# Layer 1's feed-forward: the last norm scaled with tokens on partitions instead of transposed twice

## The chip, the cores and the metric

The kernel runs on one core of one Trainium2 chip. The metric is the device time of one execution in microseconds (us), of which the profile shows the part that it calls the span. A core has a matrix engine (TensorE, PE in the profile, its weight loads PEld), a vector engine (VectorE, DVE), an activation engine (ScalarE, ACT), a general engine (GpSimd, POOL), and a queue for transfers (SP). They run side by side, each in its own program order, and wait for one another by semaphores.

## The reference

Thirty-two images of 3 x 256 x 256 go through a patch tokenizer (256 tokens of 256 features for each image), layer 0 (attention, then a feed-forward on selected tokens) and layer 1 (attention, then a feed-forward with experts). The change lies in the last: with `h` the tokens of an image, `x` its layer norm, four heads (NH) of 64 features (HD), four experts (NE) in each head:

```python
sx = einsum('bsh,ndh->bnsd', x, hl_w) + hl_b
q = einsum('bnsd,neod->bneso', sx, wq); k = einsum('bnsd,nod->bnso', sx, wk); v = einsum('bnsd,nod->bnso', sx, wv)
att = softmax(einsum('bnesd,bntd->bnest', q, k) * d ** 0.5 + causal)
qkv = einsum('bnest,bntd->bnesd', att, v)
gs = softmax(einsum('bnsf,nef->bnse', out, gate_w) + gate_b)        # out: the experts' qkv side by side
mixed = einsum('bnsed,bnse->bnsd', out, gs)
hn = layernorm(mixed + resid, ln_g, ln_b)                           # over 64 features
hx = relu(fx @ fc1_w.T + fc1_b) @ fc2_w.T + fc2_b                   # fx: hn by head
hx = layernorm(hx + fx, fnorm_g, fnorm_b)                           # the last norm
fg = softmax(fout @ fgate_w.T)                                      # fout: hx, heads side by side
result = h + fout * fg                                              # one factor of fg for each head
```

## The kernel before

All is float32, with tokens or features on the 128 partitions. An image has 256 tokens, so two chunks (NC = 2) of 128. The residual `H[b]`, two chunks by 256 features, stays in SBUF from the tokenizer to the end. The stages before layer 1's feed-forward are not touched, but for lines in `prepare`, which makes small weights in passing.

PSUM is used as eight banks of 128 x 512, handed out in turn by `bank()`: who asks for a bank waits until the reader of eight banks earlier is done.

The feed-forward is cut into 59 pieces (`PIECES`), small functions that each work on one image. `ROUND` is a list of (how many images back, piece), written out in full, and a round goes through it once; so pieces of about eight images are interleaved, and every engine gets its instructions in that order (`manual_schedule`). When the last image's scores are reached, the list `END` takes over. All instructions of one engine are thus in a fixed order, and an instruction that waits holds up all behind it on its engine. The pieces of an image:

- `tokens`: the layer norm of `H[b]` without scale and bias, two DVE instructions of 128x256 in `normed`. `turn`, `turned`: transposed by PE, copied by ACT (`exT`).
- `heads`, `heads_out`: `sx`, features on partitions; a copy `sw` with the halves of the partitions exchanged is made by DMA. `heads_zero` counts zeros in it on DVE, as (post, 16) does later in `fxT`.
- `experts`, `experts_out`: `g`, `sx` times the product of an expert's query matrix and the key matrix.
- `head_values`, `head_values_out`: the values of a head, with a few columns beside them: for each expert, EC = 5 columns, which are four for the gate's logits and one that gives the sum of the exponentials. A row of `ev` holds VC = 84 columns: 5 + 5 + 64 + 5 + 5. DVE adds a row of zeros and ones (`ones_row`) on the way from PSUM to SBUF.
- `scores` 0 to 5, `exponentials` 0 to 5 (ACT, `et`), `later_keys` 0 to 5: POOL zeroes what lies behind the causal mask (L1136).
- `outputs` 0 to 7: exponentials times values, for one head and one chunk. `TAKE` says which columns of `ev` an expert takes: 74 or 69, so that a head's four experts are 286 columns of a bank, which ACT copies to `eo` (L1153). `OWN` and `MIX` say where an expert's logits and values are in it.
- (post, 0), (post, 1): reciprocal of the sums, logits of the gate, its exponential on ACT. (post, 2): rest of the softmax on DVE, then POOL multiplies the experts' values by the gates, two instructions of 128x1024 (L1215). (post, 3): DVE adds the experts (`two`, `er`) and the residual. (post, 15), (post, 4): squares on ACT, their sums on DVE, and POOL's power −1/2 (`head_rstd`, L1167). (post, 5): `er` times that (L1233).
- (post, 6), (post, 60): transposed, scaled (`fxT`). (post, 7), (post, 70): first layer, Relu. (post, 8), (post, 80): second layer, with four more columns for each head that carry the logits of the last gate, to `ey`, tokens on partitions, by DVE. (post, 9), (post, 10): squares, sums, power as above.
- (post, 11): `enorm`, `ey` times the power (L1273); the logits of the gate, and its exponential on ACT (`fgate`).
- (post, 12): four transposes of `enorm`; (post, 120): ACT scales and shifts by feature, `foT` (L1286); (post, 13): four transposes back (L1294).
- (post, 14): rest of the gate's softmax (L1178 to L1180), the transposed norm in PSUM times the gate (L1300), plus `H[b]` (L1304), and the DMA to the output.

So the last norm's scale and bias, which go by feature, are applied where features lie on partitions, between two transposes:

```python
im.fT = p1.tile([P, 2, N], F32, name="foT")
nc.scalar.activation(
    im.fT.rearrange("p k n -> p (k n)"), im.pt, AF.Identity, bias=col("fn_b"), scale=col("fn_g")
)
```

Of the kernel before, what the change touches and what calls it, by code (L numbers as in the profile page):

```python
# [33 lines left out]
F32 = mybir.dt.float32  # L34
AF = mybir.ActivationFunctionType
# [44 lines left out]
def vit_tower(tc, a, out):  # L80
# [468 lines left out]

    EC = NE + 1  # L550
    VC = NE * EC + HD
    TAKE = ((0, 2 * EC + HD), (EC, EC + HD), (2 * EC, EC + HD), (2 * EC, 2 * EC + HD))
    OC = sum(w for _, w in TAKE)

    starts = [sum(w for _, w in TAKE[:e]) for e in range(NE)]
    OWN = [starts[e] + (0, EC, 2 * EC + HD, 3 * EC + HD)[e] - TAKE[e][0] for e in range(NE)]
    MIX = [starts[e] + 2 * EC - TAKE[e][0] for e in range(NE)]

# [63 lines left out]
    def prepare():  # L622
# [13 lines left out]
        for o in (NE, EC + NE, 2 * EC + HD + NE, 3 * EC + HD + NE):  # L636
            nc.gpsimd.memset(ones_row[:, o : o + 1], 1.0)
# [38 lines left out]
        for hp in range(2):  # L676
            for k, o in enumerate((0, 2 * EC + HD)):
                w = WV[:, hp, o : o + 2 * EC].rearrange("p (e x) -> p e x", e=2)
                nc.gpsimd.memset(w[:, :, NE:], 0.0)
                nc.vector.tensor_copy(  # L680
                    w[:, :, 0:NE],
                    pv[:, hp * 16 + k * 8 : hp * 16 + k * 8 + 8].rearrange("p (e x) -> p e x", e=2),
                )
# [27 lines left out]
        for hp in range(2):  # L711
            nc.vector.tensor_copy(WV[:, hp, 2 * EC : 2 * EC + HD], wv_i[:, hp, :])
# [39 lines left out]

    def normed_e(pool, b):
        x = pool.tile([P, NC, D], F32, name="ex")
        normed(x, b, st_e)
        return x

    def features(pool, x):
        xT = pool.tile([P, 2, N], F32, name="exT")
        nc.scalar.copy(xT.rearrange("p k n -> p (k n)"), feature_major(x))  # L760
        return xT
# [250 lines left out]
    with (  # L1012
# [13 lines left out]
        def tokens(b, im):  # L1026
            im.x = normed_e(p1, b)
# [70 lines left out]
        def head_values_out(b, im):  # L1098
            im.v = p2.tile([P, NC, NH, VC], F32, name="ev")
            for h, p in enumerate(im.pv):  # L1100
                nc.vector.tensor_tensor(
                    im.v.rearrange("p c (k h) x -> p (c k) h x", h=2)[:, :, h, :],
                    p[:, 0 : 2 * NC * VC].rearrange("p (g x) -> p g x", x=VC),
                    over(ones_row, [P, 2 * NC, VC], 1), ALU.add,
                )

# [34 lines left out]
        def outputs(b, im, j):  # L1141
            if j == 0:
                im.o = p2.tile([P, NC * NH, 360], F32, name="eo")
            n, c = ((0, 0), (1, 0), (0, 1), (1, 1), (2, 0), (3, 0), (2, 1), (3, 1))[j]
            p, o = bank(), 0
            for e in range(NE):
                x, w = TAKE[e]
                for m in range(c + 1):
                    t = im.t[n, e, True] if m else im.t[n, e, False][:, c * P : (c + 1) * P]
                    for q in (slice(0, HD), slice(HD, P)):  # L1150
                        mm(p[q, o : o + w], t[:, q], im.v[:, m, n, x : x + w], m == 0, m == c)
                o += w
            nc.scalar.copy(im.o[:, c * NH + n, 0:OC], p[:, 0:OC])  # L1153
# [33 lines left out]
        def expert_pair(im, k, at, w):  # L1187

            x, step = at[2 * k], at[2 * k + 1] - at[2 * k]
            return im.o[:, :, x : x + 2 * step].rearrange("p g (e x) -> p g e x", e=2)[:, :, :, 0:w]  # L1190

        def post(b, im, i):
# [78 lines left out]
            if i == 11:  # L1271
                im.r = p1.tile(G8, F32, name="enorm")
                nc.vector.tensor_tensor(im.r, im.y[:, :, 0:HD], over(im.rs, G8, 2), ALU.mult)  # L1273
                lg = spool.tile([P, NC, NH, NH], F32, name="lg2")
                nc.vector.tensor_tensor(
                    lg.rearrange("p c n x -> p (c n) x"), im.y[:, :, HD:], over(im.rs, [P, NC * NH, NH], 2), ALU.mult
                )
                im.gate = spool.tile([P, NC, NH], F32, name="fgate")
                nc.vector.tensor_reduce(im.gate, lg.rearrange("p c n x -> p c x n"), AX.X, ALU.add)
                nc.vector.tensor_tensor(im.gate, im.gate, over(fg_row, [P, NC, NH], 1), ALU.add)  # L1280
                softmax_to_exp(im.gate, NC)
            if i == 12:
                im.pt = feature_major(im.r.rearrange("p (c n) d -> p c (n d)", c=NC))
            if i == 120:
                im.fT = p1.tile([P, 2, N], F32, name="foT")
                nc.scalar.activation(  # L1286
                    im.fT.rearrange("p k n -> p (k n)"), im.pt, AF.Identity, bias=col("fn_b"), scale=col("fn_g")
                )
            if i == 13:
                im.po = bank()  # L1290
                for c in range(NC):
                    for k in range(2):
                        o = c * D + k * P
                        nc.tensor.transpose(im.po[:, o : o + P], im.fT[:, k, c * P : (c + 1) * P], ident)  # L1294
            if i == 14:
                softmax_rest(im.gate, NC)

                y = p1.tile([P, NC, D], F32, name="ex" if b > B - 6 and b % 2 else "fout")
                y8 = y.rearrange("p c (n d) -> p (c n) d", d=HD)
                nc.vector.tensor_tensor(  # L1300
                    y8, im.po.rearrange("p (g d) -> p g d", d=HD),
                    over(im.gate.rearrange("p c n -> p (c n)"), G8, 2), ALU.mult,
                )
                nc.vector.tensor_tensor(y, y, H[b], ALU.add)  # L1304
# [10 lines left out]
            (tokens,), (turn,), (turned,), (heads,), (heads_out,), (experts, 0), (head_values,), (experts_out, 0),  # L1315
            (experts, 1), (experts_out, 1), (head_values_out,), (scores, 0), (scores, 1), (exponentials, 0),
            (exponentials, 1), (heads_zero,), (later_keys, 0), (scores, 2), (scores, 3), (scores, 4), (scores, 5),
            (exponentials, 2), (exponentials, 3), (exponentials, 4), (later_keys, 1), (exponentials, 5),
            (later_keys, 2), (later_keys, 3), (outputs, 0), (outputs, 1), (outputs, 2), (outputs, 3),
            (later_keys, 4), (outputs, 4), (outputs, 5), (later_keys, 5), (outputs, 6), (outputs, 7), (post, 0),  # L1320
            (post, 1), (post, 2), (post, 3), (post, 15), (post, 4), (post, 5), (post, 6), (post, 60), (post, 16),
            (post, 7), (post, 70), (post, 8), (post, 80), (post, 9), (post, 10), (post, 11), (post, 12), (post, 120),
            (post, 13), (post, 14),
        )
        ROUND = (
            (1, 39), (0, 24), (0, 25), (-3, 0), (-1, 13), (4, 54), (3, 48), (4, 55), (0, 26), (0, 27), (3, 49),
            (-1, 14), (2, 44), (2, 45), (5, 57), (1, 40), (5, 58), (-2, 3), (2, 46), (-1, 15), (-3, 1), (4, 56),
            (-2, 4), (0, 28), (0, 29), (-3, 2), (0, 30), (0, 31), (3, 50), (3, 51), (1, 41), (0, 32), (0, 33),
            (0, 34), (0, 35), (3, 52), (0, 36), (3, 53), (0, 37), (-2, 5), (-2, 6), (-1, 16), (-2, 7), (0, 38),
            (-2, 8), (-2, 9), (-1, 17), (-1, 18), (-2, 10), (1, 42), (-1, 19), (-1, 20), (2, 47), (-1, 21), (1, 43),  # L1330
            (-1, 22), (-1, 23), (-2, 11), (-2, 12),
        )
        END = (
            (3, 47), (0, 21), (0, 22), (2, 43), (5, 57), (5, 58), (0, 23), (4, 54), (2, 44), (3, 48), (3, 49),
            (0, 24), (1, 39), (0, 25), (2, 45), (2, 46), (0, 28), (0, 29), (1, 40), (0, 26), (1, 41), (2, 47),
            (0, 30), (0, 27), (0, 32), (0, 31), (0, 33), (0, 34), (1, 42), (0, 35), (0, 36), (3, 50), (1, 43),
            (3, 51), (0, 37), (3, 52), (2, 48), (2, 49), (0, 38), (0, 39), (1, 44), (1, 45), (1, 46), (4, 55),
            (0, 40), (3, 53), (4, 56), (0, 41), (3, 54), (4, 57), (2, 50), (1, 47), (2, 51), (1, 48), (1, 49),
            (0, 42), (0, 43), (4, 58), (0, 44), (3, 55), (2, 52), (2, 53), (0, 45), (3, 56), (3, 57), (3, 58),
            (0, 46), (1, 50), (0, 48), (1, 51), (0, 47), (1, 52), (0, 49), (2, 54), (2, 55), (2, 56), (2, 57),  # L1340
            (1, 53), (0, 50), (1, 54), (2, 58), (0, 51), (0, 52), (1, 55), (0, 53), (1, 56), (1, 57), (1, 58),
            (0, 54), (0, 55), (0, 56), (0, 57), (0, 58),
# [411 lines left out]
```

## Time and profile before

| | |
|---|---|
| median of 3 runs | 1951.76 us (1950.18 to 1952.43) |
| the profiled execution | 1953.11 us, span 1951.4 us, mean clock 0.989 |
| busy in the span: PE, PEld | 1908.1 us (98%), 1370.5 us (70%) |
| DVE, ACT, POOL | 1209.3 us (62%), 821.0 us (42%), 877.5 us (45%) |
| from 1240 us on: layer 1's feed-forward | some 710 us |

The shares are means over stages. In the part that the change touches, the feed-forward from about 1240 us to the end, all engines are busier than over the span. Times of instructions are from the profile: a group's mean is the duration of one instruction, but instructions of one engine overlap at their ends, so that the distance from start to start, read from the timeline, is what one costs its engine.

### The profile page before, as it was taken

To read this page: it belongs to the slowest core of one execution; us is meant where nothing else is said; L and a number is where in the kernel's file an instruction comes from. 1 tells how busy PE (TensorE), PEld (TensorE's weight loads), DVE (VectorE), ACT (ScalarE), POOL (GpSimd) and SP (SyncE) were. 2 spreads that over 40 slices of the span, in tenths; PEclk is the share of its full clock that TensorE was granted. 3 is DMA by queue.
4 is the path that set the end of the run, shared out by engine and by line. 5 is a ranking of instruction groups with operands and counts; after the bars stand their busy time and mean duration, and the time that the engine had idled before them with its cause. 6 is when DMAs were issued, how large, how long until landed. Compare 5 with 4: busy or idle time off the path is not lost.

```text
span 1951.4 us, 37903 instructions
## 1 busy us (share of the span) xinstructions
PE 1908.1 (98%) x15108; PEld 1370.5 (70%) x15108; DVE 1209.3 (62%) x3225; ACT 821.0 (42%) x1549; POOL 877.5 (45%) x1072
## 2 busy tenths in 40 slices
PE   9999999999999999999989999999999999999994
PEld 7887676767676767676545555577888888888873
DVE  2334456565656574434365655545788888888886
ACT  0001222121212122212434444367878787878762
POOL 1224224343424252433443343336767676767672
PEclk9999999999999999999999999999999999999996
DMA  8540000000000042221000000011222222222212
GB/s 289 161 148 15 1 17 30 19 22 11 22 12 22 33 140 57 81 62 52 17 11 1 1 1 1 1 23 29 52 55 56 56 54 58 53 60 51 62 51 61
DMA packets 69671, 95.03 MB, mean 49 GB/s; under 512 B 8561, under 2 KB 51057, under 8 KB 69105
## 3 DMA queue, kind: packets, MB, share of 16 engines
q1 hardware_dynamic: 62768, 74.98, 13.4%
q0 software_dynamic: 6144, 16.79, 2.8%
q8 instruction: 121, 1.98, 0.4%
q10 hardware_dynamic: 576, 0.79, 0.1%
q14 instruction: 62, 0.50, 0.1%
HBM read 46.38 MB, written 20.97 MB: 35 GB/s over the span
## 4 chain that ended last, share of the span: by engine, by line
PE 95%; DVE 2%; POOL 1%; DMA 1%; ACT 0%; issue 0%; SPq 0%; ACTq 0%; DVEq 0%
PE bank L115 90%; PE bank L750 2%; PE bank L188 1%; PE bank L1294 1%; DMA patch<-in_patches_dram 0%; POOL hv L1167 0%; PE bank L229 0%; PE bank L482 0%; POOL et L1136 0%; DVE six L123 0%; DMA both<-hx 0%; POOL eo L1215 0%; DVE enorm L1273 0%; DVE ranges L1228 0%; DVE h L827 0%
## 5 line engine op out<-in xcount | busy, mean ns | idle before, releaser
L1136 POOL TENSOR_SCALAR_AFFINE_SELECT et<-et 128x256 f32<-128x256 f32 (+1 forms) x384 | 200.2, 553 | 19.4 <-ACT et L1126 18.8
L115 PE MATMUL bank<-ev,et 128*64 128x74 f32 (+1 forms) x6144 | 205.7, 227 | 1.9 <-POOL et L1136 1.9
L115 PEld LDWEIGHTS bank<-ev,et 128*64 128x64 f32 x6144 | 197.6, 138 | 8.0 <-issue 5.2
L1126 ACT ACTIVATE et<-bank 128x512 f32<-128x512 f32 x384 | 201.0, 660 | 0.0
L115 PE MATMUL bank<-tokW,patch 128*128 128x256 f32 x768 | 169.1, 383 | 2.7 <-DMA patch<-in_patches_dram 2.7
L115 PE MATMUL bank<-g,sx 64*128 64x512 f32 (+1 forms) x512 | 170.7, 483 | 0.0
L115 PE MATMUL bank<-g,sw 64*128 64x512 f32 (+1 forms) x512 | 170.3, 483 | 0.0
L115 PEld LDWEIGHTS bank<-tokW,patch 128*128 128x128 f32 x768 | 147.7, 193 | 24.4 <-issue 3.5
L1153 ACT COPY eo<-bank 128x286 f32<-128x286 f32 x256 | 101.9, 402 | 91.1 <-PE bank L115 78.7
L115 PE MATMUL bank<-bxT,w_wuv 128*128 128x512 f32 x300 | 131.4, 592 | 0.0
L115 PEld LDWEIGHTS bank<-g,sw 64*128 64x128 f32 x512 | 95.7, 187 | 33.0 <-issue 21.9
L148 POOL TENSOR_SCALAR rs_c<-st_c 128x4 f32<-128x4 f32 x16 | 3.1, 191 | 251.8 <-DVE st_c L124 251.8
L1215 POOL TENSOR_TENSOR eo<-eo,gate 128x1024 f32<-128x1024 f32 x60 | 115.2, 1940 | 1.5 <-DVE gate L1212 1.5
L115 PE MATMUL bank<-wvo,dm 128*128 128x512 f32 x256 | 114.3, 599 | 0.0
L115 PE MATMUL bank<-attn,bv 128*128 128x256 f32 x512 | 113.1, 379 | 0.0
L115 PE MATMUL bank<-w_wo,gT 128*128 128x256 f32 x512 | 113.1, 379 | 0.0
L115 PE MATMUL bank<-w_w,hT 128*128 128x256 f32 x512 | 113.1, 379 | 0.0
L115 PE MATMUL bank<-xsel,w_w 128*128 128x512 f32 x256 | 111.4, 592 | 0.0
L1167 POOL TENSOR_TENSOR hv<-hv,minus_half 128x8 f32<-128x8 f32 x64 | 108.8, 1699 | 5.3
L115 PEld LDWEIGHTS bank<-attn,bv 128*128 128x128 f32 x512 | 97.2, 190 | 19.6 <-issue 6.9
L115 PEld LDWEIGHTS bank<-g,sx 64*128 64x128 f32 x512 | 95.7, 187 | 19.4 <-issue 14.8
L123 DVE BATCH_NORM_STATS2 six<-h 128x6 f32<-128x256 f32 x256 | 105.6, 412 | 4.4
(268 smaller groups left out, 3845.6 us busy)
## 6 DMA issues: line engine op xcount, KB each, us to landing
patch<-in_patches_dram SPq DMA_DIRECT2D x31, 768.0 KB, 4.6
sw<-sx SPq DMA_DIRECT2D x64, 128.0 KB, 2.7
both<-fxT SPq DMA_DIRECT2D x64, 128.0 KB, 3.2
both<-hx SPq DMA_DIRECT2D x64, 128.0 KB, 2.4
out_dram<-fout SPq DMA_DIRECT2D x29, 256.0 KB, 2.1
cs<-ranked SPq DMA_DIRECT2D x32, 128.0 KB, 2.0
results<-cy SPq DMA_DIRECT2D x32, 128.0 KB, 1.7
w_w<-in_w_dram SPq DMA_DIRECT2D x2, 1024.0 KB
```

Source lines behind the costliest of these rows:

```text
L115: nc.tensor.matmul(o, lhsT, rhs, start=first, stop=last)
L123: nc.vector.bn_stats(six, x)
L148: nc.gpsimd.tensor_scalar(o, var, 1.0, 1e-5, ALU.mult, ALU.add)
L188: nc.tensor.transpose(p[:, o : o + P], x[:, c, k * P : (k + 1) * P], ident)
L750: nc.tensor.transpose(p[:, o : o + P], x[:, c, k * P : (k + 1) * P], ident)
L1126: nc.scalar.activation(t, p, AF.Exp)
L1136: nc.gpsimd.affine_select(out=own, in_=own, pattern=[[0, n_e], [1, P]], compare_op=ALU.is_ge, fill=0.0, base=0, channel_multiplier=-1,)
L1153: nc.scalar.copy(im.o[:, c * NH + n, 0:OC], p[:, 0:OC])
L1167: nc.gpsimd.tensor_tensor(v, v, minus_half, ALU.pow)
L1215: (nc.vector if b > B - 3 else nc.gpsimd).tensor_tensor(im.mix[k], im.mix[k], over(im.gate[:, :, 2 * k : 2 * k + 2], [P, NC * NH, 2, HD], ...
L1294: nc.tensor.transpose(im.po[:, o : o + P], im.fT[:, k, c * P : (c + 1) * P], ident)
```

## The change

The last norm stays with tokens on partitions. (post, 12), (post, 120) and (post, 13) are gone, and (post, 11) makes no `enorm`. (post, 14) makes, after the gate's softmax, the product of gate and power (`both_factors`, 128x8); then for each of the eight combinations of chunk and head one DVE instruction of 128x64 that multiplies `ey` by its column of `both_factors` and by the row `fn_g`; eight more that multiply the row `fn_b` by the gate and add `H[b]`; and one addition of 128x512 of the two.

The values have a second copy: a row of `ev` is 148 columns (5 + 64 + 5, twice), so that every expert takes 69 columns (WC) and a head's four are 276. `head_values` and its 84 columns in PSUM are as before; `head_values_out` is now three DVE additions (4x74, 4x5, 4x5) and one ACT copy of 4x64 for each of two banks. `MIX` is such that the values of two experts lie side by side in `eo`.

`tokens` runs on ACT (two instructions of 128x256 with scale and bias by token), after one small DVE instruction for the bias (`e_less`).

`PIECES`, `ROUND` and `END` are new. In `ROUND`, (post, 14) follows closely on (post, 2), (post, 80) comes behind it, and `tokens` between them:

```diff
     EC = NE + 1
+    WC = EC + HD
     VC = NE * EC + HD
-    TAKE = ((0, 2 * EC + HD), (EC, EC + HD), (2 * EC, EC + HD), (2 * EC, 2 * EC + HD))
-    OC = sum(w for _, w in TAKE)
...
+    VU = 2 * (WC + EC)
+    TAKE = (0, EC, WC + EC, WC + 2 * EC)
+    OC = NE * WC
...
         def tokens(b, im):
-            im.x = normed_e(p1, b)
+            im.x = p1.tile([P, NC, D], F32, name="ex")
...
+            nc.vector.scalar_tensor_tensor(less, st[:, i, :, 0], -1.0, rs, ALU.mult, ALU.mult)
+            for c in range(NC):
+                nc.scalar.activation(
+                    im.x[:, c, :], H[b][:, c, :], AF.Identity, bias=less[:, c : c + 1], scale=rs[:, c : c + 1]
+                )
...
         def head_values_out(b, im):
-            im.v = p2.tile([P, NC, NH, VC], F32, name="ev")
+            im.v = p2.tile([P, NC, NH, VU], F32, name="ev")
             for h, p in enumerate(im.pv):
...
+                first = WC + EC
                 nc.vector.tensor_tensor(
...
+                    v[:, :, 0:first], p[:, :, 0:first], over(ones_row[:, 0:first], [P, 2 * NC, first], 1), ALU.add
                 )
+                nc.vector.tensor_tensor(
+                    v[:, :, first : first + EC], p[:, :, first : first + EC],
+                    over(ones_row[:, first : first + EC], [P, 2 * NC, EC], 1), ALU.add,
+                )
+                nc.vector.tensor_tensor(
+                    v[:, :, VU - EC :], p[:, :, first + EC :], over(ones_row[:, first + EC :], [P, 2 * NC, EC], 1), ALU.add
+                )
+                nc.scalar.copy(v[:, :, first + EC : VU - EC], p[:, :, EC:WC])
...
             if i == 11:
-                im.r = p1.tile(G8, F32, name="enorm")
-                nc.vector.tensor_tensor(im.r, im.y[:, :, 0:HD], over(im.rs, G8, 2), ALU.mult)
...
-            if i == 12:
-                im.pt = feature_major(im.r.rearrange("p (c n) d -> p c (n d)", c=NC))
-            if i == 120:
...
-            if i == 13:
...
             if i == 14:
                 softmax_rest(im.gate, NC)
...
+                nc.vector.tensor_tensor(both, gate, im.rs, ALU.mult)
+                z = p1.tile(G8, F32, name="enorm")
...
+                for g in range(NC * NH):
+                    nc.vector.scalar_tensor_tensor(
+                        z[:, g, :], im.y[:, g, 0:HD], both[:, g : g + 1], row_e("fn_g"), ALU.mult, ALU.mult
+                    )
+                for g in range(NC * NH):
+                    c, n = g // NH, g % NH
+                    nc.vector.scalar_tensor_tensor(
+                        y[:, c, n * HD : (n + 1) * HD], row_e("fn_b"), gate[:, g : g + 1],
+                        H[b][:, c, n * HD : (n + 1) * HD], ALU.mult, ALU.add,
+                    )
                 nc.vector.tensor_tensor(
-                    y8, im.po.rearrange("p (g d) -> p g d", d=HD),
-                    over(im.gate.rearrange("p c n -> p (c n)"), G8, 2), ALU.mult,
+                    y, y, z.rearrange("p (c n) d -> p c (n d)", c=NC), ALU.add
                 )
-                nc.vector.tensor_tensor(y, y, H[b], ALU.add)
                 nc.sync.dma_start(out[b].rearrange("(c p) d -> p c d", p=P), y)
```

The new round, as (images back: piece), from the fourth entry before (post, 14) to (post, 3), and its end:

```
1:post2  0:outputs1  -1:exponentials0  4:post14  0:outputs2  0:outputs3  0:outputs4  3:post8  2:post6  2:post60
-3:tokens  -2:heads  -2:heads_out  3:post80  3:post9  2:post16  -1:later_keys0  -1:heads_zero  -1:scores1  1:post3
-1:exponentials1  -1:later_keys1  -1:scores2  0:outputs5  -1:outputs0  -1:exponentials2  0:outputs6  3:post10
...
0:post0  3:post11      then, at the head of the next:  1:post1  -1:head_values_out  0:scores4  2:post5
0:exponentials4  0:scores5  -1:scores0  0:exponentials5  0:later_keys4  0:later_keys5
```

## The prediction

> **What bounds the kernel now.** I read the stretches first, then the groups by line and shape inside the steady part, then who waited for whom, then the timelines of VectorE and GpSimd. Stretches of 100 us (busy us of PE, PEld, DVE, ACT, POOL; granted clock; DMA):
>
> ```profile
> 1400.00:1500.00 100.00, 100.00 (x1592) 81.80 (x1591) 85.68 (x200) 79.37 (x174) 70.49 (x93) 1.00 0.22 55
> 1600.00:1700.00 100.00, 100.00 (x1581) 80.85 (x1578) 86.43 (x205) 80.06 (x177) 71.12 (x94) 1.00 0.22 55
> ```
>
> The reader is to see PE without a gap at full clock, and DVE at 86%. The chain of waits repeats one piece at a fixed distance:
>
> ```profile
> 1469.35 16.09 PE bank L115 x290
> 1488.92 16.09 PE bank L115 x290
> ```
>
> 1488.92 − 1469.35 = **19.57 us: one image, one pass of ROUND**. Such pieces stand from 1352 to 1841 us: 26 full rounds. Each us per round is worth 26 us of the end.
>
> Groups of 1300 to 1800 us (25.5 rounds): line, engine, out<-in, count | busy us, mean ns | idle before.
>
> ```profile
> L115 PE MATMUL bank<-ev,et 128*64 128x74 f32 x2456 | 123.2, 229 | 0.3 <-POOL et L1136 0.3
> L115 PE MATMUL bank<-ev,et 128*64 128x69 f32 x2464 | 109.1, 223 | 1.6 <-POOL et L1136 1.6
> L1215 POOL TENSOR_TENSOR eo<-eo,gate 128x1024 f32<-128x1024 f32 x51 | 97.2, 1925 | 1.5 <-DVE gate L1212 1.5
> L1180 DVE TENSOR_TENSOR fgate<-fgate,sm_m 128x8 f32<-128x8 f32 x22 | 42.7, 1939 | 0.7
> L1304 DVE TENSOR_TENSOR fout<-fout,h 128x512 f32<-128x512 f32 x21 | 33.3, 1584 | 0.7
> L1233 DVE TENSOR_TENSOR er<-er,hv 128x512 f32<-128x512 f32 x25 | 28.3, 1133 | 1.8 <-POOL hv L1167 1.8
> L1273 DVE TENSOR_TENSOR enorm<-ey,hv 128x512 f32<-128x512 f32 x23 | 15.7, 683 | 0.0
> L1173 DVE TENSOR_TENSOR fgate<-fgate,sm_m 128x8 f32<-128x8 f32 x23 | 3.8, 167 | 0.8
> ```
>
> Two products of the same shape, 8 elements wide: 167 ns at L1173, 1939 ns at L1180. Two 512 wide: 683 and 1584. The long ones wait inside their own duration. The two timelines (start us, us) show for what; of DVE:
>
> ```profile
> 1489.43 1.58 DVE L1304 TENSOR_TENSOR fout<-fout,h 128x512 f32<-128x512 f32 x1
> ...
> 1506.25 1.94 DVE L1180 TENSOR_TENSOR fgate<-fgate,sm_m 128x8 f32<-128x8 f32 x1
> ```
>
> and of POOL:
>
> ```profile
> 1506.23 3.81 POOL L1215 TENSOR_TENSOR eo<-eo,gate 128x1024 f32<-128x1024 f32 x2
> ```
>
> L1180 starts 0.02 us after POOL's first product with the gates and ends with it; L1304, a round later, waits for the second. This **hidden stall** is (1.94−0.17) + (1.58−0.68) + (1.13−0.68) + some 0.2 at small products = 3.3 us a round. DVE also idles openly (who waited for whom: us in total, times, longest):
>
> ```profile
> DVE ey L1265 <- PE bank L115: 30.3, 23, 5.2
> DVE ranges L1228 <- ACT esq L1184: 24.3, 25, 1.6
> ```
>
> 30.3/25.5 + 24.3/25.5 = 2.1, with small waits 2.3. So DVE's own work, gaps between dependent instructions included, is 19.57 − 3.3 − 2.3 = 14.0 us.
>
> **What the Trainium skill says.** "SBUF — State Buffer", Who interferes with whom: a VectorE instruction with two SBUF inputs and a GpSimd instruction that reads SBUF exclude one another for the whole instruction. The 1.94 against 0.17 us agrees; L1300, with one input in PSUM, runs beside the same POOL product in 0.69. "VectorE: DVE Perf Modes", Rules for kernel authors: the number of chained VectorE instructions is what to keep small. Here 32 elements take 184 ns and 512 take 683: 1.04 ns an element and 0.15 us fixed. "PSUM — Partial Sum Buffer", Specifications: eight banks; the kernel takes all eight in turn, so a late reader stops PE eight banks on. No stall of this kind is in the steady trace of before.
>
> **Part by part, us per round.**
>
> *PE.* Gone: four transposes of `enorm` and four of `foT`, each four 0.44 from start to start: −0.88. Half of the 192 output matmuls go from 74 to 69 columns: 123.2/2456 against 109.1/2464 is 5.9 ns counted alone, but the two forms overlap; from start to start a pair takes 59 against 56 ns: 48 × 3.2 ns = −0.15. PE's floor becomes 19.57 − 1.03 = **18.54**. If the width is not what sets these matmuls, 18.69.
>
> *ACT.* Gone `foT` (start to start 0.66). Added: two normalisations 128x256 (nearest L1059, 0.61, the second 0.37 after the first: 0.8) and two copies of values 128x256 (nearest the `eo` copies, 0.40: 0.75). 15.7 + 0.9 = 16.6: below PE's floor by sum, so I cost it at nothing; the cover goes if ACT is held up, see the third rival.
>
> *POOL.* The same instructions, 13.8 busy.
>
> *DVE.* Gone: `ex` 2 × 0.33, `enorm` 0.60, the gate product from PSUM 0.73: −2.0. `both_factors` +0.2, `e_less` +0.15. Values: two additions of 296 instead of 336 elements, four of 20 at 0.1 each: +0.3. Sixteen products with a pointer scalar, 64 wide. The nearest row is 256 wide:
>
> ```profile
> 1181.56 1.66 DVE L955 SCALAR_TENSOR_TENSOR h<-bank,d_rs,h 128x256 f32<-128x256 f32 x4 [0.84 <-POOL d_rs L149]
> ```
>
> (1.66 − 0.48)/3 = 0.39 from start to start, less 192 × 1.04 ns is 0.19; sixteen are 3.1. Bounds: 0.14 (the second of two 64-wide products at L1201 starts that much after the first), so 2.3; 0.26 if they do not overlap, so 4.2. The last addition replaces L1304's. Sum +1.75: DVE's own work is **15.7** (14.9 to 16.8).
>
> *Stalls.* The instructions on DVE that read two SBUF operands grow by some twenty, and the order puts (post, 14) right behind DVE's part of (post, 2), whose gate starts POOL's two products of 1.92. Behind that gate DVE has a reduction and a reciprocal, 0.4, then only two-input instructions: `fgate`, `both_factors`, sixteen products, the addition. So most of 3.85 is lost: 3.3. Where DVE and POOL both queue, the traces show them alternating (L1233 goes between two selects), so the two selects of (later_keys, 0) that follow cost the products 2 × 0.36 = 0.7; `er` by `hv` 0.45 as now; small products and `two` against other selects 0.5. Sum 5.0 (3.0 to 6.0). The two open waits on PE and ACT disappear, since DVE is now late for them; the wait of (post, 11) for POOL's power, 1.69 after the reduction with some 1.6 of DVE work between, and the wait for ACT's square come to 0.8.
>
> *The round* is 15.7 + 5.0 + 0.8 = **21.5: DVE sets it, not PE**. PE meets it at bank reuse: the banks of (post, 8) wait for (post, 80), which is behind (post, 14) on DVE, and (outputs, 5) takes them again.
>
> *Queues.* On SP the output's DMA waits for the end of (post, 14), and `sw<-sx` stands behind it; its reader is a round on and it lands in 2.7, so nothing. POOL's order behind the products is selects needed half a round on: nothing. `prepare` makes some more small copies and memsets beside a PE that is busy: nothing.
>
> *Fill and drain.* The first rounds have no late pieces: 0. In the drain DVE is the longest engine already (35.6 of the last 52 us): three images × 1.75 more, less the transposes' chain of the last image (from 1940.6 to 1943.8, some 3): +3.
>
> Sum: 26 × (21.5 − 19.57) + 3 = +53 on the profiled execution's 1953.1, which is 1.3 over the median 1951.8: **2005**.
>
> **Rivals.** (1) *PE stays the bound.* DVE's stalls and waits together stay under 18.54 − 15.7 = 2.8 a round; break-even is 3.9. POOL's products must then fall beside the counts of zeros and the PSUM additions instead of the products. 26 × 1.03 = −27, so 1925. For: both engines' sums are below 18.6. Against: 3.3 is lost now with half as many such instructions. (2) *DVE binds mildly*: products at 0.14, and a run of them keeps POOL out instead of alternating: 14.9 + 3.9 + 0.9 = 19.7; with the drain +6, so 1958. (3) *ACT's order adds a loop*: its normalisation waits for `e_less`, which is behind (post, 14) on DVE. From there to the end of (exponentials, 5) ACT has 13.2 of its own, at the start-to-start times of its timeline (five pairs of exponentials at 1.0, four copies of `g` 2.0, four of `eo` 1.6, two squares 1.1, normalisations, `sx` and values 0.8 each, the rest 1.1); then POOL's select 1.3, its products 3.9, DVE's rest of (post, 14) 4.1: 22.5, +79, so 2031. (4) *Narrower matmuls bring nothing*: 4 us at most, inside the others.
>
> **How the numbers follow.** 0.2% (3.9 us) is about what a measurement of this kernel tells from no change. The forecast (rounds of 20.6 to 22.4) has 0.50, rival 1 0.15, rival 2 0.22 (of it 0.03 faster, 0.05 the same), rival 3 0.13. So faster 0.18, same 0.05, slower 0.77. The slower cases' own range is 1960 to 2035; taking in rival 2's fast side (round 19.4) gives 1948 to 2035, leaving out rival 1 and the worst of rival 3.
>
> **What would show it.** Right: rounds of about 21.5 us, PE with gaps of 2 to 3 us a round ahead of (outputs, 5) released by DVE `ey`; one `fgate`, `both_factors` or `enorm` instruction of 1 to 2 us in each round; DVE near 98%. Wrong: PE at 100% and a round of 18.5, or these products all at their short duration; then the stalls were mispriced. `enorm` rows with a step of 0.14 or 0.26 would show that I mis-sized the product.

## The result, and the profile after

The changed kernel takes **2013.93 us** (median of 4 runs, 2012.07 to 2015.08) against 1950.97 us of the kernel before on the same chip (4 runs, 1949.97 to 1952.43): a ratio of 1.0321, with an interval of 1.0303 to 1.0339. The profiled execution has a span of 2013.3 us, 61.9 more than before, and a mean clock of 0.977.

The stretches of the kernel after (us of PE, PEld, DVE, ACT, POOL; granted clock; DMA share; GB/s), one of the steady part and the last one:

```profile
1500.00:1600.00 100.00, 89.80 (x1383) 70.12 (x1383) 92.80 (x269) 72.95 (x171) 61.92 (x82) 0.98 0.22 55
...
1950.00:2014.00 64.00, 20.70 (x300) 15.47 (x296) 48.37 (x175) 10.65 (x24) 14.36 (x15) 0.61 0.17 47
```

PE now has gaps, 10 us in 100, and does 1383 matmuls in 100 us of the steady part where it did 1592. DVE has gone from 86% to 93%. The page's shares of the chain that ended last say the same for the whole span (PE had 95% and DVE 2% before):

```profile
PE 71%; DVE 22%; ACT 4%; issue 1%; POOL 0%; DMA 0%; SPq 0%; ACTq 0%; DVEq 0%; POOLq 0%
```

In the chain of waits of the kernel after (start us, us, what), the piece that repeats is no longer a run of matmuls but (post, 14) on DVE:

```profile
1430.68 5.98 DVE enorm L1297 x8
...
1444.49 0.59 ACT esq L1191
1445.11 0.69 DVE ranges L1236
...
1452.72 5.26 DVE enorm L1297 x8
...
1474.05 5.26 DVE enorm L1297 x8
...
1481.67 0.36 DVE ey L1273
1482.17 5.79 PE bank L115 x98
...
1495.44 5.07 DVE enorm L1297 x5
```

1495.44 − 1430.68 is 64.76 us for three images, 21.6 for one. The eight products take up to 5.98 us. The two lines after the third of them show how DVE holds PE: the addition (post, 80) at L1273 comes behind (post, 14), and PE's output matmuls come behind that addition. In the two rounds before, the chain comes back to DVE through ACT instead, from the normalisation behind `e_less` to a square and its sum (`esq`, `ranges`). That is the loop of rival 3, which "The loop of `e_less`" below looks into. Groups of the kernel after, 1300 to 1800 us (line, engine, out<-in, count | busy us, mean ns | idle before):

```profile
L1297 DVE SCALAR_TENSOR_TENSOR enorm<-ey,both_factors,rows_e 128x64 f32<-128x64 f32 x161 | 112.2, 764 | 0.7
L1302 DVE SCALAR_TENSOR_TENSOR fout<-rows_e,fgate,h 128x64 f32<-128x64 f32 x160 | 32.9, 273 | 0.0
L1306 DVE TENSOR_TENSOR fout<-fout,enorm 128x512 f32<-128x512 f32 x20 | 13.8, 692 | 0.7
L1187 DVE TENSOR_TENSOR fgate<-fgate,sm_m 128x8 f32<-128x8 f32 x21 | 9.8, 467 | 0.7
```

L1297 and L1302 are the same instruction in shape, and one takes 764 ns, the other 273. `fgate` (1939 ns before) and the last addition (1584 before) are now at 467 and 692: most of the stall has moved from them to the products. Why is in the timelines of one round of the kernel after (start us, us); DVE's:

```profile
1516.92 0.62 DVE L1187 TENSOR_TENSOR fgate<-fgate,sm_m 128x8 f32<-128x8 f32 x1
1517.57 0.55 DVE L1292 TENSOR_TENSOR both_factors<-fgate,hv 128x8 f32<-128x8 f32 x1
1518.16 5.26 DVE L1297 SCALAR_TENSOR_TENSOR enorm<-ey,both_factors,rows_e 128x64 f32<-128x64 f32 x8
1523.35 1.64 DVE L1302 SCALAR_TENSOR_TENSOR fout<-rows_e,fgate,h 128x64 f32<-128x64 f32 x8
```

and POOL's:

```profile
1518.08 3.96 POOL L1223 TENSOR_TENSOR eo<-eo,gate 128x1024 f32<-128x1024 f32 x2
1521.99 0.77 POOL L1142 TENSOR_SCALAR_AFFINE_SELECT et<-et 128x256 f32<-128x256 f32 x2
```

From 1518.08 to 1522.76 POOL has two products and two selects, and DVE's first eight products last for all of it. Taken singly, they go 1909, 272, 1929, 433, 436, 272, 272 and 272 ns, beside POOL's 1913 and 1970 (products) and 406 (selects): DVE waits out one POOL instruction, gets one product in, and waits out the next. Where nothing is in the way, products start 0.196 us apart.

### The profile page after: what moved, and what is told of

It reads as the page before. It is cut to its first block, busy times and chain, and to the rows that moved or that the text cites. A ratio compares the mean times of both kernels' runs of the same rounds, so it can differ in the third digit from the quotient of the medians.

```text
span 2013.3 us, 37927 instructions
## 1 busy us (share of the span) xinstructions
PE 1903.8 (95%) x14852; PEld 1350.2 (67%) x14852; DVE 1351.9 (67%) x3805; ACT 833.3 (41%) x1645; POOL 881.9 (44%) x1076
## 4 chain that ended last, share of the span: by engine, by line
PE 71%; DVE 22%; ACT 4%; issue 1%; POOL 0%; DMA 0%; SPq 0%; ACTq 0%; DVEq 0%; POOLq 0%
PE bank L115 69%; DVE enorm L1297 8%; DVE fout L1302 2%; ACT et L1132 1%; PE bank L188 1%; DVE er L1241 1%; DVE ev L1101 1%; DVE fout L1306 1%; ACT eo L1160 1%; ACT esq L1191 1%; DVE ranges L1236 1%; DVE fgate L1187 1%; DVE both_factors L1292 1%; ACT sx L1056 1%; DVE sm_m L1186 1%
## 5 line engine op out<-in xcount | busy, mean ns | idle before, releaser
L1142 POOL TENSOR_SCALAR_AFFINE_SELECT et<-et 128x256 f32<-128x256 f32 (+1 forms) x384 | 206.3, 563 | 193.9 <-ACT et L1132 191.0
L115 PEld LDWEIGHTS bank<-ev,et 128*64 128x64 f32 x6144 | 208.4, 146 | 91.2 <-issue 75.7
L115 PE MATMUL bank<-ev,et 128*64 128x69 f32 x6144 | 217.2, 234 | 54.8 <-DVE ey L1273 54.8
L1132 ACT ACTIVATE et<-bank 128x512 f32<-128x512 f32 x384 | 210.0, 628 | 2.5 <-PE bank L115 2.5
L115 PE MATMUL bank<-g,sw 64*128 64x512 f32 (+1 forms) x512 | 185.4, 492 | 0.0
L115 PE MATMUL bank<-g,sx 64*128 64x512 f32 (+1 forms) x512 | 185.0, 492 | 0.0
L1297 DVE SCALAR_TENSOR_TENSOR enorm<-ey,both_factors,rows_e 128x64 f32<-128x64 f32 x256 | 156.8, 681 | 1.1
L115 PEld LDWEIGHTS bank<-g,sx 64*128 64x128 f32 x512 | 90.7, 187 | 32.8 <-issue 22.9
L115 PEld LDWEIGHTS bank<-w_w,hT 128*128 128x128 f32 x512 | 96.6, 190 | 15.3 <-issue 2.9
```

The lines of the kernel that those rows point to most:

```text
L115: nc.tensor.matmul(o, lhsT, rhs, start=first, stop=last)
L1132: nc.scalar.activation(t, p, AF.Exp)
L1142: nc.gpsimd.affine_select(out=own, in_=own, pattern=[[0, n_e], [1, P]], compare_op=ALU.is_ge, fill=0.0, base=0, channel_multiplier=-1,)
L1297: nc.vector.scalar_tensor_tensor(z[:, g, :], im.y[:, g, 0:HD], both[:, g : g + 1], row_e("fn_g"), ALU.mult, ALU.mult)
```

## The experiments

"Round" is the distance of two images in the steady part of the trace. The stall is summed over DVE's instructions in it: duration less the shortest one of the same form (same operation, same sizes). All ratios are to the kernel before on the same chip.

| kernel | median us | ratio (interval) | round | stall |
|---|---|---|---|---|
| before | 1951 | | 19.57 | 3.6 |
| after | 2013.93 | 1.0321 (1.0303 to 1.0339) | 21.6 | 5.1 |
| tokens_early | 2015.86 | 1.0327 (1.0310 to 1.0344) | 21.7 | |
| norm_alone | 2010.09 | 1.0301 (1.0283 to 1.0318) | 21.4 | 5.9 |
| norm_by_powers | 2043.01 | 1.0473 (1.0455 to 1.0490) | 22.9 | 2.1 |
| norm_by_powers2 | 2012.71 | 1.0314 (1.0297 to 1.0332) | 21.6 | 3.2 |
| mix_short2 | 1939.16 | 0.9951 (0.9934 to 0.9968) | 19.0 | 1.8 |
| rest_alone | 1962.78 | 1.0059 (1.0042 to 1.0076) | 19.8 | |
| wide_norm | 1992.20 | 1.0219 (1.0202 to 1.0236) | 20.9 | 5.4 |
| values_on_dve | 1948.36 | 0.9980 (0.9969 to 0.9990) | 19.4 | |
| mix_dve | 1976.73 | 1.0127 (1.0112 to 1.0143) | 20.2 | 1.6 |
| wide_mix_dve | 1955.61 | 1.0021 (1.0013 to 1.0029) | 19.55 | 1.6 |
| wide_reordered | 1958.21 | 1.0043 (1.0029 to 1.0057) | 19.7 | 1.7 |

Theory 1 is the prediction's: the round is DVE's, by its own work and by its stalls against POOL. What stands against it in the expectations below is theory 2 (DVE's own work sets the round without the stalls), theory 3 (rival 3: the loop of ACT's normalisation behind `e_less`) and theory 4 (the other parts of the change cost).

### Only the last norm: norm_alone

The kernel before, its order and all else kept, with (post, 12), (post, 120) and (post, 13) gone and the new (post, 14) in its old place (three buffers for `ey`, six for `hv`, since both are held longer):

```diff
-            if i == 12: ...          (and 120, 13)
+            if i == 14:              (the softmax, both_factors, 8 + 8 products, one addition, as after)
```

> The kernel before, with only the last norm changed: no transposes, sixteen products and one addition in (post, 14), three buffers for `ey`; the round, the end, `tokens` on DVE, `ev` and the 74 columns as before. Theory 1: DVE's own work 14.0 - 1.3 + 3.3 = 16.0, stalls 4.9 since (post, 14) stands behind (post, 2) here too, waits 0.5: a round of 21.4, some 2001 us (1985 to 2015). Theory 4 (what costs is the new round, or `tokens` on ACT, or the values' second copy): at most 1955, and 1926 if PE still sets the round at 18.7.

2010.09 us, 21.4 a round: this part alone makes all but 4 us of the loss. A stretch of norm_alone, and groups from 1300 to 1800 us:

```profile
1500.00:1600.00 100.00, 93.63 (x1314) 72.45 (x1311) 97.04 (x257) 70.79 (x156) 61.51 (x85) 0.98 0.21 52
```

```profile
L1289 DVE SCALAR_TENSOR_TENSOR enorm<-ey,both_factors,rows_e 128x64 f32<-128x64 f32 x160 | 87.6, 615 | 0.7
L1284 DVE TENSOR_TENSOR both_factors<-fgate,hv 128x8 f32<-128x8 f32 x20 | 37.5, 1875 | 0.7
```

In the old order the first of POOL's products is waited out in `both_factors` (8 elements, 1875 ns), the second in the products. The sum is not smaller for it, 5.9 against 5.1: the stall belongs to whatever two-input instructions stand behind the gate. The run also speaks against theory 3: it has no `e_less`, and the normalisation is DVE's. DVE is at 97%, and the chain of waits from 1400 to 1500 us is made of DVE's instructions alone.

### The other parts: rest_alone and values_on_dve

rest_alone is the kernel before with all of the change but the last norm: the second copy of the values, 69 columns for every expert, values copied and tokens normalised by ACT, all in the old order of pieces.

```diff
-                im.v = p2.tile([P, NC, NH, VC], F32, name="ev")
+                im.v = p2.tile([P, NC, NH, VU], F32, name="ev")
...
+                nc.scalar.copy(v[:, :, first + EC : VU - EC], p[:, :, EC:WC])
```

> The kernel after's other parts without the last norm: values with a second copy, 69 columns for each expert, `tokens` on ACT; the last norm, the pieces, the round and the end as in the kernel before. Theory 1: PE 0.2 us a round less and still without a gap, DVE 0.2 less, ACT 1.5 more but under PE: 1944 to 1950. Theory 4 (these parts cost): above 1960.

A miss: 1962.78 us, slower than before by 0.6%, 19.84 a round. The output matmuls did get 0.19 us a round shorter (6.11 to 5.92 from start to start), but PE lost more than that elsewhere: 0.2 ahead of `heads`, 0.1 within it and 0.2 among the matmuls of the scores. The stretch of rest_alone has ACT at 84%, where it was 79 to 80% before:

```profile
1500.00:1600.00 100.00, 99.81 (x1596) 81.11 (x1592) 77.15 (x215) 84.00 (x192) 68.63 (x90) 1.00 0.23 55
```

values_on_dve tests that: the same, but with the copy and the normalisation on DVE, which has room in the kernel before.

```diff
-                nc.scalar.copy(v[:, :, first + EC : VU - EC], p[:, :, EC:WC])
+                nc.vector.tensor_copy(v[:, :, first + EC : VU - EC], p[:, :, EC:WC])
```

(and `normed` on DVE for `tokens`, as before)

> The kernel before with the values' second copy and 69 columns for each expert, the copy made by DVE instead of ACT; `tokens`, last norm, pieces, round and end as before. In rest_alone PE's output matmuls took 0.19 us a round less and PE lost 0.3 behind ACT. Theory 1: DVE gets 1.0 us a round more (2 x 0.33 and four narrow additions), of 2.3 that it idles; PE stays without a gap, a round of 19.38: 1944 to 1948. If DVE is not free at the places where these stand: 1952 to 1965.

1948.36 us, 0.2% under before (interval 0.9969 to 0.9990), with rounds of 19.38 (a mean of 19.46, since one in eight is 20.1). So narrower output matmuls, with the copy that they need on DVE, are worth some 3 us, and by the two ratios some 15 us lie between the copy and the normalisation on DVE and the same on ACT. Which of the two pieces costs this on ACT was not separated. Of the versions that compute the whole result it is the one that beats both kernels, by about as much as the measurement can tell.

### Without POOL's products: mix_short2

POOL's products are cut short, so that DVE meets next to nothing of them. The kernel leaves out the gates of 63 of 64 columns, and (post, 3) adds `H[b]` to itself in place of the experts' values, with the same sizes and two operands in SBUF; so its output is not the model's, and only its time is of use. (mix_short, with the first of these two edits alone, has no time: some results of the unweighted values were not finite.) All else is as after.

```diff
-                        im.mix[k], im.mix[k], over(..., [P, NC * NH, 2, HD], 3), ALU.mult
+                        im.mix[k][:, :, :, 0:1], im.mix[k][:, :, :, 0:1], over(..., [P, NC * NH, 2, 1], 3), ALU.mult
-                nc.vector.tensor_tensor(two, im.mix[0], im.mix[1], ALU.add)
+                nc.vector.tensor_tensor(two, h8, h8, ALU.add)        # h8: H[b], in the shape of two
```

> The kernel after, but POOL's product of the experts' values with the gates covers 1 of 64 columns, and (post, 3) adds H to itself in place of the experts' values (same shape, same two SBUF operands), so that all numbers stay small. Theory 1 (POOL's two products of 1.9 us hold off the sixteen small products of (post, 14)): the stall inside `enorm` falls from 3.9 us a round to under 1, the round from 21.6 to 18.5 to 19.2 us, the time to 1925 to 1945. Theory 2 (DVE's longer own work sets the round by itself): the round stays above 20.5, the time above 1985.

1939.16 us, 75 less than after, with DVE's instructions the same in number, shape and order. Stretch, group and two pieces of the chain of waits of mix_short2:

```profile
1500.00:1600.00 100.00, 100.00 (x1588) 78.11 (x1584) 87.67 (x306) 85.22 (x192) 50.72 (x90) 1.00 0.22 58
```

```profile
L1299 DVE SCALAR_TENSOR_TENSOR enorm<-ey,both_factors,rows_e 128x64 f32<-128x64 f32 x184 | 60.0, 393 | 0.8
```

```profile
1452.71 10.24 PE bank L115 x180
...
1471.73 10.24 PE bank L115 x180
```

The products are at 393 instead of 764 ns, and PE is without a gap. The chain of waits of the steady part is PE's throughout, so the round of 19.0 is PE's own. Theory 2 falls with it. Theory 3 does not: POOL's products are a member of rival 3's loop too. They took 0.24 us each here, 3.4 less in all, and 22.5 less 3.4 is 19.1. Against it stands norm_alone, and the next run tests that loop in the new order.

### The loop of `e_less`: tokens_early

```diff
 ROUND, as (images back: piece):
-        1:post2  0:outputs1  -1:exponentials0  4:post14  ...  2:post60  -3:tokens  -2:heads
+        -3:tokens  1:post2  0:outputs1  -1:exponentials0  4:post14  ...  2:post60  -2:heads
```

> The kernel after with one piece moved in the round: `tokens` stands ahead of (post, 2), so that `e_less` is no longer behind (post, 14) on DVE and ACT does not wait for it (4 us a round in the kernel after). Theory 1: ACT's wait is a consequence; the round stays at 21.7 and the time within 6 us of 2014. Theory 3 (the loop through `e_less`, ACT, the exponentials and POOL sets the round): 1 us a round or more is gained, 1990 or less.

2015.86 us, no gain. In the waits of after (engine line waited for: us in total, times, longest) the normalisation stands high; it is a wait of ACT, 1300 to 1850 us:

```profile
ACT ex L1022 <- DVE e_less L1020: 100.1, 23, 5.3
PE bank L115 <- DVE ey L1273: 43.3, 22, 2.9
DVE ranges L1236 <- ACT esq L1191: 20.5, 23, 2.6
```

In tokens_early the first line is gone. ACT now waits for `ey` of (post, 80), which stands behind the same (post, 14) on DVE:

```profile
ACT esq L1191 <- DVE ey L1273: 73.8, 22, 4.2
PE bank L115 <- DVE ey L1273: 44.4, 22, 2.9
```

So ACT is still held by DVE, and this run takes only one entrance of the loop away. How much ACT's lateness can cost is in the third line of after: DVE stands idle for ACT's squares 20.5 us in some 25 rounds, 0.8 us a round, and in the steady part, apart from 0.5 for PE at `ev` and the gaps between dependent instructions, it is never without an instruction. A round longer by 2.1 us than before cannot come from 0.8. ACT's wait was slack behind DVE, not what set the round; PE's wait for `ey` is as long as it was.

### POOL's products on DVE: mix_dve, wide_norm, wide_mix_dve

mix_dve gives the two products with the gates to DVE, which has the most to do already. It is the sharpest test of the stall: DVE's own work rises by more than 2 us a round.

```diff
-                    (nc.vector if b > B - 3 else nc.gpsimd).tensor_tensor(
+                    nc.vector.tensor_tensor(
```

> The kernel after with the two products of values and gates on DVE for every image, nothing else. Theory 1: DVE's own work 16.1 + 2.3 = 18.4, stalls against the selects 1.0 to 1.8, waits 0.5: a round of 19.9 to 20.7, 1962 to 1985, faster than the kernel after although DVE has more to do. Theory 2: 21.6 + 2.3, above 2060.

1976.73 us, 37 less than after, with more work on the engine that bounds. Groups of mix_dve, 1300 to 1800 us:

```profile
L1223 DVE TENSOR_TENSOR eo<-eo,gate 128x1024 f32<-128x1024 f32 x50 | 71.3, 1426 | 1.7
L1297 DVE SCALAR_TENSOR_TENSOR enorm<-ey,both_factors,rows_e 128x64 f32<-128x64 f32 x176 | 38.8, 287 | 0.8
```

The two products cost DVE 2.85 a round, what they wait for included, and the eight products of `enorm` are back at 287 ns. The stall goes from 5.1 to 1.6, and the gaps between DVE's instructions from 1.7 to 1.4; with 1.4 less for the round that leaves 2.4 more of own work.

wide_norm takes the other term, DVE's own work: five 512-wide instructions instead of sixteen products and an addition.

```diff
-                for g in range(NC * NH):
-                    nc.vector.scalar_tensor_tensor(z[:, g, :], im.y[:, g, 0:HD], both[:, g : g + 1], row_e("fn_g"), ALU.mult, ALU.mult)
-                for g ...                                      (fn_b times the gate, plus H[b])
+                nc.vector.tensor_tensor(z, im.y[:, :, 0:HD], over(both, G8, 2), ALU.mult)
+                nc.vector.tensor_tensor(y8, over(row_e("fn_b"), G8, 1), over(gate, G8, 2), ALU.mult)
+                nc.vector.tensor_tensor(z, z, over(row_e("fn_g"), G8, 1), ALU.mult)
+                nc.vector.tensor_tensor(y, y, H[b], ALU.add)
```

> The kernel after with the sixteen products of 64 columns and the addition as five instructions of 512 columns: 0.6 to 0.7 each against 16 x 0.196 + 0.75. Theory 1: DVE's own work 0.7 us a round less, and as DVE sets the round, so is the round, with stalls of 4 to 5 as before: 20.6 to 21.2, 1985 to 2003. If the number of instructions queued against POOL sets the stall (fewer hand-overs): down to 19.8, 1965. Theory 3 (a loop through ACT sets it): 2010 or more.

1992.20 us, 20.86 a round, 0.77 less than after. The stall stays, 5.4; now it sits in the first two of the five:

```profile
L1298 DVE TENSOR_TENSOR fout<-rows_e,fgate 128x512 f32<-128x512 f32 x21 | 49.0, 2335 | 0.0
L1297 DVE TENSOR_TENSOR enorm<-ey,both_factors 128x512 f32<-128x512 f32 x21 | 48.5, 2311 | 0.7
```

So DVE's own work taken away comes off the round, and fewer instructions do not make the stall smaller: two are enough to wait out POOL's two. wide_mix_dve does both at once:

```diff
-                    (nc.vector if b > B - 3 else nc.gpsimd).tensor_tensor(          (products with the gates)
+                    nc.vector.tensor_tensor(
-                for g in range(NC * NH): ...                                    (sixteen products)
+                nc.vector.tensor_tensor(z, im.y[:, :, 0:HD], over(both, G8, 2), ALU.mult)   ... as in wide_norm
```

> wide_norm with the two products of values and gates on DVE for every image instead of on POOL. Theory 1: DVE's own work 16.1 - 0.75 + 2.3 = 17.7, stalls only against POOL's selects, 1.0 to 1.5, waits 0.5: a round of 19.0 (PE, as mix_short2 shows) to 19.7, so 1935 to 1958. Theory 2 (own work alone counts, stalls are filled in from other waits): 20.86 + 2.3, 2045 or more.

1955.61 us, 19.55 a round: 0.2% above before (interval 1.0013 to 1.0029), and none of PE's saving left, with DVE at 93% from 1500 to 1600 us.

### Other places for (post, 14): norm_by_powers, norm_by_powers2, wide_reordered

norm_by_powers puts (post, 14) behind (post, 4) of three images later, beside POOL's powers, and (post, 80) with the zero counts beside POOL's products:

```diff
 ROUND, the stretches with moved pieces:
+        1:post2  -1:scores0  0:exponentials5  0:later_keys4  0:later_keys5  3:post8  2:post6  2:post60
+        0:outputs1  -1:exponentials0  3:post80  0:outputs2 0:outputs3 0:outputs4  -3:tokens  2:post16  -1:heads_zero
+        -2:heads  -2:heads_out  3:post9
...
+        0:outputs5  -1:outputs0  3:post10  1:post15  -1:exponentials2  0:outputs6  1:post4  4:post14  0:outputs7
-            v = spool.tile([P, NC * NH], F32, name="hv")
+            v = spool.tile([P, NC * NH], F32, name="hv", bufs=4)
```

> The kernel after with another round, all pieces as they are: (post, 2) earlier, POOL's products ahead of (later_keys, 4); (post, 80) and the counts of zeros behind (post, 2), beside POOL's products; (post, 14) behind (post, 4), so that its products run beside POOL's two powers; (post, 8), (post, 6), (post, 15), (post, 10) moved to suit. Four buffers for `hv`. Theory 1: the powers do not hold off DVE, so stalls fall from 5.1 to some 2 a round, and the round to 18.6 to 19.4: 1928 to 1950. Theory 2 (DVE's own work): above 20.5 a round, 1985 or more. A new wait that I have not seen, between the two: 1950 to 1985.

A miss: 2043.01 us. The stall did fall, from 5.1 to 2.1 a round; waits took its place. Of norm_by_powers, 1300 to 1850 us:

```profile
POOL eo L1223 <- DVE gate L1220: 91.4, 23, 4.2
DVE ranges L1236 <- ACT esq L1191: 75.4, 46, 2.9
PE bank L115 <- DMA both<-hx: 37.9, 38, 2.0
```

The last of these is a queue: the output's DMA now stood ahead of the copy `both` on SP. norm_by_powers2 mends that and gives `esq` a second buffer:

```diff
-        3:post10  1:post15  -1:exponentials2  0:outputs6  1:post4  4:post14  0:outputs7  2:post7  2:post70
+        1:post15  -1:exponentials2  0:outputs6  3:post10  1:post4  0:outputs7  2:post7  2:post70  4:post14
-            sq = p1.tile(G8, F32, name="esq")
+            sq = p1.tile(G8, F32, name="esq", bufs=2)
```

> As norm_by_powers, mended where its trace shows new waits: the output's DMA stands behind the two `both` DMAs on SP instead of ahead of them, and `esq` has two buffers, so that the second square does not wait for the first one's sum. Theory 1: stalls stay near 2 a round, the waits for `both` (38 us between 1300 and 1850 us) and for squares (75 us) shrink, the round falls from 22.9 to 18.6 to 19.8: 1930 to 1960. If some other wait of this order sets it: above 22 still, 2020 or more.

2012.71 us, again a miss: a stall of 3.2, and a loop in its place. The idea behind the order did hold. POOL's power, 1.64 us long, does not hold the products off: of DVE, then of POOL,

```profile
1549.44 1.67 DVE L1297 SCALAR_TENSOR_TENSOR enorm<-ey,both_factors,rows_e 128x64 f32<-128x64 f32 x8
...
1549.45 1.64 POOL L1174 TENSOR_TENSOR hv<-hv,minus_half 128x8 f32<-128x8 f32 x1
```

and eight products in 1.67 us are eight at their short distance, 7 x 0.196 + 0.27. The loop is in the chain of waits, here over two images (start us, us, what):

```profile
1520.24 4.19 POOL et L1142 x5
...
1529.51 2.49 DVE fout L1302 x8
...
1541.83 4.19 POOL et L1142 x5
...
1551.11 2.49 DVE fout L1302 x8
```

POOL's selects let PE's output matmuls go, ACT copies and squares, DVE sums and goes through (post, 14). From there the chain comes back to POOL's next selects, once through the values, PE and ACT's exponentials, once through the gate and POOL's products: 21.6 us around, without DVE being full (83% in the stretch from 1500).

wide_reordered is wide_mix_dve with `tokens` ahead of (post, 2), (post, 8) behind (outputs, 2), and (post, 80) ahead of (post, 14):

```diff
-        1:post2  0:outputs1  -1:exponentials0  4:post14  0:outputs2 0:outputs3 0:outputs4  3:post8  2:post6  2:post60  -3:tokens  -2:heads  -2:heads_out  3:post80
+        -3:tokens  1:post2  0:outputs1  -1:exponentials0  0:outputs2  3:post8  3:post80  4:post14  0:outputs3 0:outputs4  2:post6  2:post60  -2:heads  -2:heads_out
```

> wide_mix_dve with three pieces moved in the round: `tokens` ahead of (post, 2); (post, 8) behind (outputs, 2); (post, 80) ahead of (post, 14). In wide_mix_dve the chain goes through DVE's (post, 14), then ACT's `ex`, `sx`, squares, exponentials, and back to DVE. Theory 1 with this loop: neither `e_less` nor `ey` stands behind (post, 14) any more, ACT is not held up, the round falls from 19.55 to 19.0 (PE) to 19.3: 1936 to 1949. If DVE's own work of 17.7 with its stalls is full by itself: 19.5 still, 1952 to 1958.

1958.21 us: no gain over wide_mix_dve. Shares of the chain that ended last, wide_reordered:

```profile
PE 70%; DVE 27%; ACT 1%; issue 1%; POOL 0%; DMA 0%; SPq 0%; DVEq 0%; ACTq 0%; POOLq 0%
```

The steady part of that chain is DVE's nearly throughout, as the other side of its expectation had it: with the products on DVE it is the sum of DVE's work that counts, and this change of order gained nothing. PE shows 99.97 to 100.00 us busy in each 100 us of the steady part here, at 19.7 a round, and does the same matmuls in 19.0 in mix_short2. So PE at 100% is no proof that PE sets the round; the chain of waits tells the two apart.

## Why the prediction was right, and where it was off

- **DVE sets the round, not PE.** Predicted 21.5 us, measured 21.6. mix_dve shows the bound from one side (most of the stall taken away, 37 us less in spite of more work), mix_short2 from the other (75 us less, PE full).
- **DVE's own work.** Predicted 15.7, measured 21.6 − 5.1 − 1.0 = 15.5. The price read off the 256-wide row, 0.19 from start to start, is 0.196. In wide_norm the round fell by 0.77 where the expectation took 0.7 off this term.
- **The stalls.** Predicted 5.0, measured 5.1, of it 3.9 in the eight products, 0.3 each in `fgate` and `both_factors`. The main part fell where the prediction put it: both POOL products and then both selects are waited out. That the sums agree to 0.1 is in part luck. `er` by `hv` lost 0.2 where 0.45 stood, and `fgate` and `both_factors` lost 0.6 to selects ahead of POOL's products, which the prediction had not put there. "SBUF — State Buffer", Who interferes with whom, in the Trainium skill, was the ground for it, and the trace bears it out with 1909 ns for a product of 272.
- **The open waits.** Predicted 0.8, measured 1.0: `ranges` behind ACT's squares (11.9 us in 18 rounds) and `ev` behind PE (5.7). Of the two that the prediction named, ACT's square is there; the wait for POOL's power is not, and `ev` has its place.
- **PE meets it at bank reuse.** The gap is ahead of (outputs, 5), and its releaser is `ey`, as said; the timeline of PE after has

```profile
1526.28 0.91 PE L115 MATMUL bank<-ev,et 128*64 128x69 f32 x23 [2.92 <-DVE ey L1273]
```

- **Narrower matmuls** were put at 0.15 a round; measured 0.13 to 0.19.
- **DVE near 98%** was not seen, 93% was. Of a round of 21.6, 1.0 are open waits, which left 95% at most (96% by the prediction's own sum), and 0.7 are gaps between dependent instructions, which are counted in its own work but not as busy.

Two terms and one cover were off.

- **The sum, 9 us short.** The distances of the experts' gates from image to image give it: over 26 rounds the mean is 21.65 against 19.51, which is +55.5 where the prediction had +50; fill and drain make up the other 6.4 of the 61.9, where +3 stood. Most of it is the last interval of the drain, 23.7 against 12.2 us; the first rounds and the start gave 4.3 back, the rest of the drain 0.8. The stretch from 1950 us shows DVE at 48 of 64 us and PE at 21.
- **PE's floor, 18.54.** mix_short2 has PE full at 19.0. The output matmuls and the transposes went as costed; other groups of matmuls, named by what they multiply, grew from start to start in a round: `g,sx` 2.68 to 2.82, `g,sw` 2.58 to 2.68, `W,both` 0.95 to 1.05, `exT` 1.73 to 1.82. Rival 1 would have come to some 1937 instead of 1925. Why they grow in the new order, whether by more changes between forms of tile, is not settled.
- **ACT at nothing.** The prediction named the cover: 16.6 us of ACT below PE's 18.5. By sum it holds, but rest_alone lost 0.27 a round, 12 us in all, where PE's saving should have shown. In the kernel after any such loss is hidden behind DVE. Whether it would have come up in rival 1 is not shown: mix_short2 has the same work on ACT and PE full at 19.0, and how much of what PE's groups grew by is ACT's was not separated.

Of the rivals, 3 named a real loop: `e_less` and ACT's chain lie on parts of the chain of waits. But norm_alone loses as much without that loop, tokens_early took the wait out and gained nothing, and DVE's own wait for ACT is 0.8 a round; so the loop runs along with DVE's bound and does not set it. Rival 2's picture, a run of products keeping POOL out, is refuted by the single durations: they alternate.

Open is whether some order of the pieces has PE's 19.0 with POOL's products kept on POOL. norm_by_powers shows that the stall can be halved by order, but both attempts put waits in its place.

## What to carry to other kernels

Before replacing work on a matrix engine with a string of two-input vector instructions, look for what GpSimd does at that moment: price the string not at its short durations but with each GpSimd product or select that it is to meet added in full. (GpSimd's power on eight columns cost it nothing here.) A busy share does not show this loss, which lies inside the durations; comparing two rows of the same shape does (273 and 764 ns). And an instruction that "the other engine has room for" should be costed at that engine's place in the order: here some 15 us lay between two engines that both had room by their sums.

## What the runs showed of the hardware

- In these traces DVE's instructions with two operands in SBUF and POOL's products and selects take turns, instruction by instruction, when both queue (1909, 272, 1929, 433, 436 ns for the same product). A string of short DVE instructions gained nothing by being many (a stall of 5.1 with sixteen and the addition, 5.4 with five), and POOL lost almost nothing: its second product started 0.08 us after the first one's end, one DVE product having started in between, and took 1970 instead of 1913 ns.
- Not every instruction of POOL takes part: eight products ran in 1.67 us beside a power of 1.64 us (norm_by_powers2). Why was not looked into.
- Moving 2.85 us of work a round from POOL to the bounding DVE made the kernel faster (2013.9 to 1976.7), because 3.5 us of stall a round went with it.
- A wait inside an instruction shows as busy. DVE's 93% of after hold 5.1 us a round by which its instructions are longer than the shortest of their form.
- The granted clock was 0.97 to 0.98 in the stretches of after, where PE has a gap of 1.4 to 2.9 us in each round, and 1.00 before. It does not follow from the share of gaps alone: from 1500 to 1600 us, wide_norm with PE at 91.77 us busy had 1.00, and norm_alone with 93.63 had 0.98. What sets it is open.
